# Slot lists one block ahead, layer weights in steps, and no empty openings in a sparse graph transformer

## Chip, cores and metric

The kernel runs on one core of one Trainium2 chip. The metric is device time in microseconds; before the change three runs gave 2359.41, 2360.68 and 2360.91 us, median 2360.68. The profile is one further execution, with a span of 2347.7 us. Below, PE is the matrix engine (TensorE), PEld its weight loads, DVE the vector engine, ACT the scalar engine, POOL the GpSimd engine, which here issues the gathers, and SP the engine that issues the plain DMAs.

## What is computed

Sixteen graphs share one adjacency of 1024 nodes with few edges (an edge with probability 0.0078, about 8 per row). Four layers follow each other: attention, graph attention, attention, attention. One attention layer is

```python
Q, K, V = h @ Wq, h @ Wk, h @ Wv              # 8 heads of 16
scores = Q K^T / sqrt(16), -inf where adj == 0
x = layer_norm(h + (softmax(scores) V) @ Wo + bo)
x = layer_norm(x + relu(x @ W1 + b1) @ W2 + b2)
```

and the graph attention layer takes `e = leaky(s_i + s_j)` from two projections of `h = x @ W`, a masked softmax over it, `att @ h + x`, and a layer norm. Everything is fp32.

## The kernel before

Because the adjacency is sparse, keys and values are not multiplied densely. In a setup phase (`graph`, L215 on) DVE counts the edges of every row, sorts the rows by degree, and finds for each sorted row the list of its neighbours. From then on the kernel gathers: per layer and graph group it keeps a table of 1024 rows with keys and values of 8 graphs, and fetches with indirect DMAs (L905, POOL) one table row per edge.

**Units.** There are 64 units (l, g, t), which the texts below call blocks and number from 0: 4 layers, 2 groups of 8 graphs, and 8 blocks t of 128 sorted nodes. Blocks 0 to 7 are layer 0 with the first group, 8 to 15 the second group. A block is cut into parts: 7 parts in t = 0, 5 in each other attention block. Per part DVE multiplies gathered keys with queries (L917), sums within heads (L940), and multiplies gathered values with the exponentials (L968); ACT takes the exponentials (L944); PE adds the edges of each node up with a 0/1 matrix `marks` (L984, accumulator `acc`). Once per block DVE divides (L1021, L1024; the denominators `ps` also come from L984).

**Slot lists.** Before a block can be gathered, `slots` (L382) must turn its neighbour lists into gather indices `idx` and into `marks`. `spread` (L384) does four small PE products (L387) into a PSUM bank; 18 small DVE instructions (L398 to L433) read that bank and write `idx` and `marks`.

**Tails.** Each block has two tails, one per half of its graphs (`attention_tail`, L662): transposes of o (L616), output projection (L680, L681), layer norm on ACT (L594 to L609), hidden layer (L691, ACT L700), second product (L705, L709), layer norm, transposes, and the projection into the next layer's table (L566 for the graph attention layer).

**Order of the work.** The order of instructions on each engine is fixed by the Python program: every engine executes its own in the order in which they were issued, and waits for others by semaphores. The main loop (L1110) issues DVE's part work and, between, calls `others()` three times per part, four in the graph attention layer. One such call is an *opening*. It advances the tails at a set pace, and then takes one step of the first generator in a queue: `fronts` if there are any, else `loads`, else the leisure work `slow`. In `fronts` stand slot lists, weights and the queries of the next block (L848: L868, ACT L872, L877, ACT L880); in `loads` stands `loaded` (L814), which fetches rows of x by an indirect DMA (L826, POOL) and transposes them (L616); in `slow` stands `at_leisure(1)` (L746), which projects keys and values of the second group (L616, L546) while the first group's blocks run. A step that only finds its generator at an end uses the opening up. Whatever is left in `fronts` at a block's end is issued there at once, and what is left in `slow` is issued before the first gather of block 8. PSUM results of PE rotate through a pool of four banks (`bank()`).

In the kernel before, `fronts` starts with all remaining slot lists, then the rows of block 1, then the weights of layer 0 and of the graph layer (L486 to L495 and L512 to L519); all of it must be issued within block 0. In `slots`, the products for the list after next are issued as soon as the bank has been read. The weights of layers 2 and 3 are worked on at the start of the fifth block of the layer ahead, all in one go (L1123).

Of the kernel before, what the change touches and what calls it, by code (L numbers as in the profile page):

```python
# [1 line left out]

# [1 line left out]

# [38 lines left out]
T = N // P  # L43
# [83 lines left out]
def sparse_path(ctx: ExitStack, tc: tile.TileContext, a: dict, out: bass.AP, flag):  # L127
# [254 lines left out]
    def slots():  # L382

        def spread(q):  # L384
            ps = bank([P, J, TOP])
            for j in range(J):
                nc.tensor.matmul(  # L387
                    ps[:, j, :], rep_of(j, True), lists[:, row_of(q, j), :],
                    start=True, stop=True,
                )  # L390
            return ps

        ps = spread(0)
        yield
        for q in range(T):
            for s in range(S):
                at = slice(32 * s, 32 * s + 32)
                nc.vector.tensor_copy(  # L398
                    val[at], ps[at].rearrange("p j (k s) -> p j k s", s=S)[:, :, :, s]
                )  # L400

            first, second = SHARED[q]
            for k in range(2):
                at = slice(32 * (2 + k), 32 * (3 + k))
                to, of = COUNT[q][first], S * COUNT[q][second] + k
                nc.vector.tensor_copy(val[at, first, to : to + 1], ps[at, second, of : of + 1])
            if 0 < q < T - 1:
                ps = spread(q + 1)

            def flat(v):  # L410
                return v.rearrange("p j k -> p (j k)")

            nc.vector.tensor_copy(flat(val_i), flat(val))

            for k, (by, op) in enumerate(
                ((2 * N - 1, ALU.bitwise_and), (11, ALU.logical_shift_right))
            ):
                nc.vector.tensor_scalar(flat(part), flat(val_i), by, None, op)
                nc.vector.tensor_scalar(
                    flat(idx[:, k, q]), flat(part), -1.0, float(N), ALU.mult, ALU.add  # L420
                )
            nc.vector.tensor_scalar(flat(used), flat(val), 0.0, None, ALU.is_gt)
            for j in range(J):
                c, n = MARK[q, j, 0], COUNT[q][j]
                nc.vector.tensor_tensor(
                    marks[:, c : c + n, :],
                    used[:, j, :n].rearrange("p (k o) -> p k o", o=1).to_broadcast([P, n, 32]),
                    mark32.to_broadcast([P, n, 32]),
                    ALU.mult,
                )  # L430
            for k in range(2):
                at, r = slice(64 * k, 64 * k + 64), COUNT[q][first]
                nc.vector.tensor_tensor(  # L433
                    marks[at, MARK[q, MIX, k], :],
                    used[at, first, r : r + 1].to_broadcast([64, 32]),
                    mark32[at, 0, :],
                    ALU.mult,
                )
            yield
            if q == 0:  # L440
                ps = spread(1)
                yield


    w = {}
# [12 lines left out]
    def load_weights(layer):  # L458

        t = wts.tile([P, 2 * D], F32, tag="Wkv", name="Wkv")
        nc.sync.dma_start(t[:, :D], a[f"{layer}_gnn_Wk"])
        nc.sync.dma_start(t[:, D:], a[f"{layer}_gnn_Wv"])
        w[layer, "Wkv"] = t
        yield
        for name in ATTN:
            src = a[f"{layer}_gnn_{name}"]
            if name in ("Wq", "Wo", "W1"):
                t = wts.tile([P, src.shape[1]], F32, tag=name, name=name)  # L470
                nc.sync.dma_start(t, src)
            elif name == "W2":
                t = wts.tile([P, F, D], F32, tag=name, name=name)
                nc.sync.dma_start(t, src.rearrange("(f p) d -> p f d", p=P))
            elif name == "b1":
                t = wts.tile([P, F], F32, tag=name, name=name)
                with nc.allow_non_contiguous_dma(reason="a bias, once"):
                    nc.sync.dma_start(t, src.rearrange("(f p) -> p f", p=P))
            elif name.startswith("ln") or name in ("b2", "bo"):
                t = wts.tile([P, 1], F32, tag=name, name=name)  # L480
                nc.sync.dma_start(t, src.rearrange("(p o) -> p o", o=1))
            else:
                continue
            w[layer, name] = t
        yield
        centred(w[layer, "Wo"], D)  # L486
        centred(w[layer, "W2"].rearrange("p f d -> p (f d)"), F * D)
        ps = bank([P, F])
        for f in range(F):
            nc.tensor.matmul(  # L490
                ps[:, f : f + 1], w[layer, "W1"][:, f * P : (f + 1) * P], w[layer, "b2"],
                start=True, stop=True,
            )
        nc.vector.tensor_tensor(w[layer, "b1"], w[layer, "b1"], ps, ALU.subtract)
        nc.vector.tensor_tensor(w[layer, "ln1_b"], w[layer, "ln1_b"], w[layer, "b2"], ALU.add)  # L495

# [2 lines left out]
    def load_graph_weights():  # L499
        for name in GAT[3:]:  # L500
            t = const.tile([P, 1], F32, name=name)
            nc.sync.dma_start(t, a[f"L1_gnn_{name}"].rearrange("(p o) -> p o", o=1))
            w["L1", name] = t

        nc.sync.dma_start(wg[:, :D], a["L1_gnn_W"])
        ends = const.tile([P, 2], F32, name="ends")
        for k, name in enumerate(("a_dst", "a_src")):
            nc.sync.dma_start(
                ends[:, k : k + 1], a[f"L1_gnn_{name}"].rearrange("(p o) -> p o", o=1)
            )  # L510
        yield
        ps = bank([P, P])  # L512
        nc.tensor.transpose(ps, wg[:, :D], ident)
        wgT = wts.tile([P, P], F32, tag="Wo", name="wgT")
        nc.vector.tensor_copy(wgT, ps)
        ps = bank([P, 2])
        nc.tensor.matmul(ps, wgT, ends, start=True, stop=True)
        nc.vector.tensor_copy(wg[:, D:], ps)
        centred(wg[:, :D], D)  # L519

# [293 lines left out]
    def loaded(u):  # L814

        if u >= len(units):
            return
        l, g, t = units[u]
        xs[units[u]] = inputs.tile([P, HF, GH, P], F32, tag="x", name="x")
        if l == 0:  # L820
            def fetch(h):
                if u == 0:
                    rows = twos.tile([P, GH, D], F32, tag="o", name="rows")
                else:
                    rows = ones_.tile([P, GH, D], F32, tag="q" if h else "rows", name="rows")
                nc.gpsimd.indirect_dma_start(  # L826
                    out=rows.rearrange("p g d -> p (g d)"), out_offset=None,
                    in_=a["x"].rearrange("n (k c) -> (n k) c", k=GR * HF),
                    in_offset=bass.IndirectOffsetOnAxis(ap=places[:, g, h, t : t + 1], axis=0),
                )  # L830
                return rows

            rows = fetch(0)
            yield "idle"
            yield "idle"
            turned(rows, xs[units[u]][:, 0])
            rows = fetch(1)
            yield "idle"
            yield "idle"
            turned(rows, xs[units[u]][:, 1])  # L840
            yield
            return
        nc.sync.dma_start(
            xs[units[u]].rearrange("p h g n -> p (h g n)"),
            kept[l, g][t].rearrange("p h c -> p (h c)"),
        )
# [192 lines left out]
    fronts = []  # L1039
# [18 lines left out]
    def others():  # L1058
        pace[0] += pace[1]
        while pace[0] >= 1.0:  # L1060
            advance(tails)
            pace[0] -= 1.0
        for gens in (fronts or loads or idle(),):
            if not gens:
                continue
            got = next(gens[0], "end")
            if got == "end":
                gens.pop(0)
            if got == "idle":
                advance(idle())  # L1070

    with tc.manual_schedule():
        wide = [gather_buffer() for _ in range(EDGES)]
# [30 lines left out]
            gathered(i)  # L1104
        nc.gpsimd.memset(wide[3], 0.0)
        gathered(AHEAD - 1)
        fronts.extend([rest, loaded(1)] + more)
        closing, sizes = None, ()
        begun = 0
        for i in range(len(parts) + 2):  # L1110
            here = i < len(parts)
            u = parts[i][0] if here else len(units)
            if here:
                l = units[u][0]
                if i and parts[i - 1][0] != u:
                    begun = i
                    if l + 1 < len(LAYERS) and LAYERS[l + 1][1] is ATTN:
                        if units[u][1:] == (0, 1):
                            more = load_weights(LAYERS[l + 1][0])
                            next(more)  # L1120
                            next(more)
                        if units[u][1:] == (0, 4):
                            next(more, None)  # L1123
                if is_attention(u):
                    products(i)
            if i > 1:
# [481 lines left out]
```

## Time and profile before

| engine | busy us of 2347.7 | share |
|---|---|---|
| PE matmul | 2066.7 | 88% |
| DVE | 1934.4 | 82% |
| ACT | 1530.3 | 65% |
| PE weight load | 1278.8 | 54% |
| POOL | 1084.9 | 46% |

DMA moved 636 MB, on average 271 GB/s. By slices of 58.7 us the busy tenths are not even (the page's second part):

| | slices 1 to 8 |
|---|---|
| PE | 7 5 4 7 9 9 8 8 |
| DVE | 7 8 7 7 7 8 6 6 |
| ACT | 3 2 1 5 7 7 7 7 |
| PE clock | 8 6 6 8 9 9 9 9 |
| DMA | 7 6 4 7 7 8 8 6 |

The setup phase ends at about 94 us; the third slice (117 to 176 us) lies in block 0. A block's length can be read from the times at which DVE starts L1021: block 0 closes at 186.7 us, block 1 at 235.2, block 2 at 277.5, block 7 at 500.1 and block 15 at 795.8. Rows of time give start, duration, engine, line, operation, what is written from what, size, number of merged instructions, and in brackets the idle time before it and what ended it. Rows of waits give the waiting instruction, what it waited for, the total, how often, and the longest.

### The profile page before, as it was taken

How to read it: one execution, taken by the hardware profiler on the slowest of the kernel's cores; microseconds unless marked ns; L12 is line 12 of the kernel's file. 1: busy time of each engine (PE TensorE's matmuls, PEld its weight loads, DVE VectorE, ACT ScalarE, POOL GpSimd, SP SyncE). 2: the span in 40 equal slices, each digit the busy share in tenths (PEclk: the TensorE clock that was granted, in tenths of full speed). 3: DMA queues.
4: the chain of work that ended last, by engine and by line, in shares of the span. 5: the costliest groups of instructions: out<-in, count | busy, mean ns of one | idle time of the engine just before them, and what ended most of it. 6: DMA issues, size and time to landing. Idle time of an engine off the chain costs nothing. (4 is left out here: it accounts for less than half of the span.)

```text
span 2347.7 us, 36598 instructions
## 1 busy us (share of the span) xinstructions
PE 2066.7 (88%) x13124; PEld 1278.8 (54%) x13124; DVE 1934.4 (82%) x1486; ACT 1530.3 (65%) x5057; POOL 1084.9 (46%) x754
## 2 busy tenths in 40 slices
PE   7547998879999899998899999999999989898987
PEld 6415665545655555554465665566555555455554
DVE  7877786689888677778898989889898888998884
ACT  3215777767777665565477876777767767676764
POOL 3334443344544568885333434343444445444441
PEclk8668999999999999999899999999999999999998
DMA  7647788668878889998888887888978677776760
GB/s 262 229 176 236 268 289 278 241 223 309 285 266 290 272 275 374 339 357 319 288 293 290 291 293 267 308 304 295 305 248 306 224 281 255 255 251 255 272 244 24
DMA packets 168461, 636.05 MB, mean 271 GB/s; under 512 B 38328, under 2 KB 41144, under 8 KB 119774
## 3 DMA queue, kind: packets, MB, share of 16 engines
q0 software_dynamic: 92672, 485.09, 57.7%
q1 hardware_dynamic: 75600, 148.55, 18.9%
q8 instruction: 105, 1.72, 0.3%
q14 instruction: 84, 0.69, 0.1%
HBM read 603.11 MB, written 92.34 MB: 296 GB/s over the span
## 5 line engine op out<-in xcount | busy, mean ns | idle before, releaser
L905 POOL DMA_INDIRECT e<-table,idx x600 | 879.5, 1466 | 1059.0 <-DVE pr L968 872.1
L968 DVE TENSOR_TENSOR pr<-e,ex 128x2048 f32<-128x2048 f32 (+1 forms) x336 | 689.3, 2060 | 54.0 <-ACT ex L944 32.1
L917 DVE TENSOR_TENSOR pr<-e,qr 128x2048 f32<-128x2048 f32 x204 | 460.6, 2258 | 184.5 <-DMA e<-table,idx 93.5
L984 PE MATMUL acc<-pr,marks 128*32 128x512 f32 x2656 | 536.8, 615 | 54.1 <-DVE pr L968 42.6
L940 DVE TENSOR_REDUCE sc<-pr 128x128 f32<-128x2048 f32 (+1 forms) x252 | 518.5, 2058 | 8.6
L594 ACT ACTIVATE z<-yps,root 128x128 f32<-128x128 f32 x888 | 317.4, 388 | 37.5 <-PE yps L709 20.6
L984 PEld LDWEIGHTS acc<-pr,marks 128*32 128x32 f32 x2656 | 109.3, 111 | 306.4 <-issue 216.1
L705 PE MATMUL yps<-W,f 128*128 128x128 f32 x1520 | 250.8, 282 | 9.3 <-ACT f L700 5.2
L609 ACT ACTIVATE z<-yps,rstd 128x128 f32<-128x128 f32 x888 | 254.0, 369 | 7.2
L705 PEld LDWEIGHTS yps<-W,f 128*128 128x128 f32 x1520 | 204.9, 192 | 57.3 <-ACT f L700 29.1
L546 PE MATMUL ps<-Wkv,xT 128*128 128x256 f32 x768 | 221.5, 430 | 15.9 <-ACT xT L622 9.5
L700 ACT ACTIVATE f<-ps,b 128x512 f32<-128x512 f32 x190 | 130.9, 693 | 159.6 <-PE ps L691 158.3
L880 ACT COPY qr<-ps 128x512 f32<-128x512 f32 x384 | 196.9, 599 | 44.6 <-PE ps L877 44.5
L877 PE MATMUL ps<-q,rep 32*128 32x512 f32 x768 | 174.4, 662 | 42.6 <-ACT q L872 40.9
L616 PE MATMUL ps<-ident,z 128*128 128x128 f32 x896 | 173.6, 297 | 36.4 <-ACT z L609 31.6
L944 ACT ACTIVATE ex<-sc 128x128 f32<-128x128 f32 (+1 forms) x252 | 79.7, 316 | 189.0 <-DVE sc L940 188.9
L594 ACT ACTIVATION_READ_ACCUMULATOR z<-yps,root 128x1 f32 x888 | 202.0, 227 | 0.0
L616 PEld LDWEIGHTS ps<-ident,z 128*128 128x128 f32 x896 | 113.9, 142 | 154.3 <-ACT z L609 84.3
L546 PEld LDWEIGHTS ps<-Wkv,xT 128*128 128x128 f32 x768 | 151.3, 211 | 79.8 <-ACT qr L880 24.3
L550 ACT COPY kv<-ps 128x512 f32<-128x512 f32 x176 | 103.4, 593 | 133.6 <-PE ps L546 130.7
L691 PE MATMUL ps<-x,W 128*128 128x512 f32 x384 | 188.8, 615 | 0.9 <-ACT x L624 0.9
L680 PE MATMUL yps<-Wo,oT 128*128 128x128 f32 x768 | 158.0, 288 | 9.6 <-ACT oT L622 9.6
(173 smaller groups left out, 2725.5 us busy)
## 6 DMA issues: line engine op xcount, KB each, us to landing
table<-kv SPq DMA_DIRECT2D x88, 512.0 KB, 6.9
qx<-qr SPq DMA_DIRECT2D x96, 256.0 KB, 5.3
kept<-xT SPq DMA_DIRECT2D x96, 256.0 KB, 3.3
x<-kept SPq DMA_DIRECT2D x48, 512.0 KB, 7.6
e<-table,idx POOLq DMA_INDIRECT x600, 7.8
table<-kv SPq DMA_DIRECT2D x32, 256.0 KB, 6.7
edges<-in_adj SPq DMA_DIRECT2D x8, 512.0 KB, 5.4
spare<-in_x SPq DMA_DIRECT2D x8, 512.0 KB, 7.9
```

The source lines that it names most:

```text
L546: nc.tensor.matmul(ps[:, k, :], x[:, i + k, :], w[LAYERS[l][0], "Wkv"], start=True, stop=True,)
L594: nc.scalar.activation(z[:, i, :], y[:, i, :], AF.Square, scale=D**-0.5, bias=root, accum_out=total[:, i : i + 1],)
L609: nc.scalar.activation(z[:, i, :], y[:, i, :], AF.Copy, scale=rstd[:, i : i + 1])
L616: nc.tensor.transpose(ps[:, i, :], z[:, i, :], ident)
L691: nc.tensor.matmul(ps, p["W1"][:, f * P : (f + 1) * P], x1.rearrange("p g n -> p (g n)"), start=True, stop=True,)
L705: nc.tensor.matmul(ps[:, i, :], f1[:, f, i * P : (i + 1) * P], p["W2"][:, f, :], start=(f == 0), stop=False,)
L880: nc.scalar.copy(qs[u][:, j, h * GH * D : (h + 1) * GH * D], pss[j])
L905: nc.gpsimd.indirect_dma_start(out=es[i][:, k, :], out_offset=None, in_=tables[l, g][:, :], in_offset=bass.IndirectOffsetOnAxis(ap=idx[:, ...
L917: nc.vector.tensor_tensor(prs[i][0][:, :n, :], es[i][:, :n, :ROW], qx[u].rearrange("p (o c) -> p o c", o=1) if (MIX, 0) in piece else of_p ...
L940: nc.vector.tensor_reduce(sc[:, :n, :], prs[i][0][:, :n, :].rearrange("p k (a d) -> p k a d", d=HD), mybir.AxisListType.X, ALU.add,)
L968: nc.vector.tensor_tensor(prs[i][k0 // 2][:, :m, :].rearrange("p k (a d) -> p k a d", d=d), es[i][:, k0 : k0 + m, base : base + ROW].rearr ...
L984: nc.tensor.matmul(outs[32 * j : 32 * j + 32], marks[:, mark, :], rhss, start=(chunk == mine[0]), stop=(chunk == mine[-1]),)
```

## The change

Five things are changed, all in the order of issue; the computation and the number of DVE and PE instructions of each kind stay as they are.

1. Slot lists are made a block ahead: list u + 1 is put into `fronts` at the start of block u (three steps of it, `islice(rest, 3)`), for u up to 6, instead of all lists in block 0.
2. Between the products of a list (`spread`) and the DVE instructions that read them lies one more opening. The products are no longer issued a list ahead.
3. The weights are worked on in steps: an opening is left between a product and DVE's reading of it (L490 to L494, L513 to L515, L517 to L518). For layers 2 and 3 this work is put into `fronts` instead of being issued in one go before the block's first L917.
4. Openings are dense: a generator that is at its end is dropped, and the opening goes to the next one.
5. In `loaded`, one more opening lies between the fetch of rows and their transposes, for both halves.

```diff
@@ slots
-        ps = spread(0)
-        yield
         for q in range(T):
+            ps = spread(q)
+            yield
+            if q:
+                yield
             for s in range(S):
...
-            if 0 < q < T - 1:
-                ps = spread(q + 1)
...
             yield
-            if q == 0:
-                ps = spread(1)
-                yield
@@ load_weights
+        yield
         nc.vector.tensor_tensor(w[layer, "b1"], w[layer, "b1"], ps, ALU.subtract)
@@ load_graph_weights
         nc.tensor.transpose(ps, wg[:, :D], ident)
+        yield
...
         nc.tensor.matmul(ps, wgT, ends, start=True, stop=True)
+        yield
         nc.vector.tensor_copy(wg[:, D:], ps)
@@ loaded, for both halves
             rows = fetch(0)
             yield "idle"
             yield "idle"
+            yield
             turned(rows, xs[units[u]][:, 0])
@@ others
-        for gens in (fronts or loads or idle(),):
+        while True:
+            gens = fronts or loads or idle()
             if not gens:
-                continue
+                break
             got = next(gens[0], "end")
             if got == "end":
                 gens.pop(0)
+                continue
             if got == "idle":
                 advance(idle())
+            break
@@ main loop
-        fronts.extend([rest, loaded(1)] + more)
+        fronts.extend([islice(rest, 3), loaded(1)] + more)
...
                     begun = i
+                    if u < T - 1:
+                        fronts.append(islice(rest, 3))
...
                         if units[u][1:] == (0, 4):
-                            next(more, None)
+                            fronts.append(more)
```

More of the change, by code (lines that the diff above doesn't have):

```diff
@@ L1 @@
 from contextlib import ExitStack
+from itertools import islice
 import numpy as np
@@ L839, in loaded @@
             yield "idle"
+            yield
             turned(rows, xs[units[u]][:, 1])
```

## The prediction

> **What bounds the kernel now.** I read the table of stretches first, cut where VectorE (DVE) closes a block (L1021), because the edit touches only the first sixteen blocks and two later spots. Columns: stretch, length, then busy time of PE, PEld, DVE, ACT and POOL, the granted PE clock, the DMA share and GB/s.
>
> ```profile
> 96.80:186.60 89.80, 41.01 (x181) 20.18 (x181) 75.44 (x165) 13.08 (x29) 27.58 (x19) 0.65 0.48 175
> 186.60:235.20 48.60, 40.38 (x241) 27.00 (x241) 32.40 (x19) 29.95 (x95) 19.97 (x15) 0.83 0.75 247
> 235.20:277.50 42.30, 38.02 (x254) 25.07 (x255) 32.40 (x18) 31.18 (x104) 17.77 (x13) 1.00 0.75 270
> 448.10:500.10 52.00, 40.38 (x253) 26.93 (x253) 32.59 (x19) 31.63 (x104) 15.24 (x12) 0.93 0.62 219
> 543.40:580.10 36.70, 33.86 (x230) 21.31 (x231) 32.21 (x18) 28.16 (x98) 19.66 (x14) 1.00 0.83 296
> ```
>
> Block 0 (first line) is DVE's: busy 75.4 of 89.8 us, while ACT and DMA are half empty. Blocks 2 to 6 of the first graph group (third line) take 42.3 us with DVE busy only 32.4 and PE 38.0; the same blocks of the second group (last line), which carry no leisure projection, take 36.7 with PE at 33.9 and the same DVE work. So those blocks follow PE, and DVE has about 10 us of slack in each. Block 7 (52.0) and block 1 (48.6) hold something extra.
>
> Next, the order in time of DVE in block 0 and the waits that end its idle time.
>
> ```profile
> 101.50 0.78 DVE L398 COPY little<-ps 32x24 f32<-32x24 f32 x4
> 104.39 0.38 DVE L433 TENSOR_TENSOR marks<-little 64x32 f32<-64x32 f32 x2
> 104.78 0.77 DVE L398 COPY little<-ps 32x24 f32<-32x24 f32 x4
> ...
> DVE pr L917 <- ACT qr L880: 6.6, 1, 6.6
> DVE b L494 <- PE ps L490: 4.0, 1, 4.0
> DVE wg L518 <- PE ps L517: 0.7, 1, 0.7
> ```
>
> One slot list takes 104.78 - 101.50 = 3.28 us of DVE, and seven stand in block 0. Three waits, 11.3 us, are DVE waiting for PE or ACT results whose instructions were issued only just before.
>
> Then the steady block, DVE and PE in order of time, and two waits of PE:
>
> ```profile
> 263.11 2.28 DVE L917 TENSOR_TENSOR pr<-e,qr 128x2048 f32<-128x2048 f32 x1
> 265.43 2.29 DVE L940 TENSOR_REDUCE sc<-pr 128x128 f32<-128x2048 f32 x1
> 272.25 2.29 DVE L968 TENSOR_TENSOR pr<-e,ex 128x2048 f32<-128x2048 f32 x1 [4.54 <-ACT ex L944]
> 277.55 0.56 DVE L1021 RECIPROCAL both<-ps 128x64 f32<-128x64 f32 x1 [3.00 <-PE ps L984]
> ...
> 267.93 1.91 PE L984 MATMUL acc<-pr,marks 128*32 128x512 f32 x8
> ...
> 191.55 1.08 PE L616 MATMUL ps<-ident,rows 128*128 128x128 f32 x4 [8.32 <-DMA rows<-in_x,places]
> 482.11 1.09 PE L616 MATMUL ps<-ident,rows 128*128 128x128 f32 x4 [6.76 <-DMA rows<-in_x,places]
> ```
>
> DVE runs ahead of PE by about 7 us at the block's start and then waits 7.5 us. The last two lines are the extra of blocks 1 and 7: PE stands still for rows of x that were asked for too late.
>
> **What the skill says.** "Perfetto Trace Analysis", Optimization Strategy: where the most contended engine changes over time, interleaving the regimes can pay. That is what the change does, and the table shows the two regimes. "TensorE: Matmul & The Clock Gate", The mechanism: matmuls start and end strictly in program order, so a spread put into PE's queue waits for all before it; the trace agrees (PE reaches the place of the new spread about 7 us after DVE). The same page, What's actually happening: the PE clock is halved after an idle window of about 3.4 us. Here the clock is 0.65 in block 0, and eight L984 took 3.63 us against 1.91 later. So PE work of block 0 is slow there, and PE prices from it are twice those of the busy blocks.
>
> **The change, part by part.**
>
> *Slots a block ahead.* By the built order, block 0 (cut at L1021) keeps the slot lists 1 and 2; lists 3 to 7 go one each to blocks 1 to 5. Block 0 loses 5 x 3.28 = 16.4 us of DVE, all on its bound. In a receiving block the list stands after the L968 that ended at 263.1 and before the L917 at 263.11. Its four spread matmuls stand on PE right after the accumulation of 267.93, so they run at about 269.8. Their cost: four took 1.87 us at half clock (L387), so I estimate 0.94 at full clock; bounds 0.6 (a row of four transposes, L616) and 1.87. PE is the bound there, so 0.94 is on the path, five times: +4.7. DVE waits at the list until 270.8, works to 274.1, and behind it are queued L917, L940 (to 278.6), L968 and L1021 (at about 281.2, against 277.55 + 0.94 without the list). The ex of that L940 is wanted by ACT at 275.98; ACT then idled for PE's L566 until 278.0, later plus 0.94, so it loses nothing. L1021 is 2.7 us late; its o is transposed at 282.3 + 0.94, still after it. The lateness ends in the next DVE wait (2 us for the accumulators, 10.0 us in five blocks) and the 4.5 us one. The spread holds one of four PSUM banks; its fourth successor (L566, 273.4) needs it back, and the six copies that free it end at about 272. So DVE's 3.3 us per block cost nothing, hidden in waits for PE.
>
> *Weights in steps.* In block 0 L494 and L518 get a DVE instruction of 2.3 us or more between matmul and reading: the waits of 4.0 and 0.7 go, -4. For layer 2 and 3 the step moves to an opening inside the loop. For layer 3 (L494 at 1246.85) L490 moves on PE behind an accumulation and a second product, 1.9 + 3.0 = 4.9 us, while L494 moves on DVE behind 4.6: the 2.84 us wait stays, 0. For layer 2 (L494 at 873.38) L490 moves behind an accumulation that took 3.63 us, L494 only behind 0.5 of small work: the wait grows from 1.8 to about 5. Behind it are an L968, and behind that the gather that waits for its buffer; DMA waits of 4 us follow, so I take +1.5 of the 3.1, bounds 0 and 3.
>
> *Dense openings and slots away: queries earlier.* The queries of block 1 now come one accumulation earlier in block 0, about 7 us, and the DVE wait of 6.6 for qr goes: -6.6. Against it, list 2 stands at the end of block 0 behind row transposes on a slow-clock PE: +4 (0 to 6). Block 0: -16.4 - 4 - 6.6 + 4 = -23.
>
> *One more opening before the row transposes.* In block 7 they now stand behind L705 and L691 of the other half. That is 2.7 + 1.9 = 4.6 us of PE work (the same rows in a steady block) inside the 6.76 it idled, and the clock need not fall (the L705 rows there took 4.2). DVE was held by a DMA until 481.48, and after it lost 1.65 (ex) and 3.34 (L1021) to PE: these 5.0 can go, I take -4.8. Block 8 is DVE's (42.7 of 43.3), so it keeps the lead. In block 1 the rows are asked for one gather earlier (12 gathers ahead instead of 13; the thirteenth waited 8.8 us on DVE): the 8.3 us stall goes and the block falls to the 42.3 of its neighbours, -6. Elsewhere the transposes fill the wait of L705 for ACT in one half instead of the other (0.4 us each): 0.
>
> Sum: -23 - 6 + 4.7 - 4.8 + 1.5 = -27.6, from 2360.7 to 2333.
>
> **Rivals.**
> *Block 0 finds another bound* (20%). Without the lists its parts follow at 6.9 us, each wants 2 MB of gathers, 290 GB/s, where the stage now moves 175; row transposes hold PE. For: two gathers took 10 us to land. Against: other stages move 296 to 356, and four buffers lie ahead. Then block 0 keeps half of its 23 and block 1 half of its 6: 2333 + 11.5 + 3 = 2347.
> *The work only moves* (5%). Each list costs its 3.3 us in its new block as well, and the stalls on rows stay: -16.4 - 10.6 + 16.4 + 4.7 + 1.5 = -4.4, 2356. The 10 us of DVE slack speak against it.
> *The list becomes the new wait* (9%, slower). DVE stops 6.7 us for the spread in five blocks, then works 3.3, and everything behind is late, gathers included: 5 x 10 = 50 instead of 4.7, with block 0 still -23, block 1 and 7 nothing gained, since POOL and PE wait on DVE, and 3 at layer 2: about +30, 2390; with half of it absorbed 2366. I take 2378. Against: the two DVE waits right behind the list are 7.5 us long and owed to PE anyway.
>
> **How the numbers follow.** Likeliest (66%) 2333. Its unknowns: the spread 5 x (0.6 to 1.9), list 2 (0 to 6), layer 2 (0 to 3), blocks 1 and 7 half or whole: 2318 to 2346. The range reaches into the first rival and a little beyond: 2318 to 2354. Faster by over 0.2% (under 2356) is the first two cases, 0.86; same is the third, 0.05; slower the last, 0.09.
>
> **What would show it.** Right: block 0 near 67 us with two lists in it; no wait of L917 on qr, nor of L494 there; blocks 2 to 5 about 43.2, with a DVE wait of some 7 us at L398 on L387 and shorter ones at L968 and L1021; block 7 near 47; L494 of layer 2 waiting 5 us. Wrong: blocks 1 to 5 above 45, block 0 above 75 with waits on gathers, or PE idle behind a PSUM bank that the list holds.

## The result and the profile after

The changed kernel took 2325.07 us (median of four, 2320.74 to 2332.53) against 2360.05 us (2353.03 to 2360.91) of the kernel before: a ratio of 0.9862, with a 95% interval of 0.9829 to 0.9895. Timed again later beside further kernels it took 2325.74 against 2351.28, ratio 0.9895 (0.9876 to 0.9914). The gain is thus 25 to 35 us; the two profiles differ by 28.8 us (2347.7 and 2318.9). The prediction said 2333 (2318 to 2354).

In the changed kernel most lines have moved by three: L917, L940, L968, L984, L1021 are now L920, L943, L971, L987, L1024, and the list is read at L401 and its products stand in L388. The table of stretches after, cut as before (stretch, length, busy time of PE, PEld, DVE, ACT, POOL, granted PE clock, DMA share, GB/s): block 0, block 1, block 2 and block 7.

```profile
97.25:169.80 72.55, 38.46 (x179) 18.12 (x179) 60.40 (x76) 14.05 (x31) 28.57 (x19) 0.74 0.61 229
169.80:213.20 43.40, 40.92 (x255) 26.49 (x252) 35.19 (x36) 30.64 (x100) 16.94 (x12) 0.93 0.75 266
213.20:254.90 41.70, 39.44 (x263) 26.03 (x260) 35.46 (x37) 31.13 (x104) 16.92 (x12) 1.00 0.78 275
420.00:465.90 45.90, 39.64 (x264) 26.14 (x262) 32.39 (x18) 32.63 (x111) 15.25 (x10) 1.00 0.69 250
```

Block 0 is 17.3 us shorter, block 1 5.2, block 7 6, and a block that now has a list in it is 0.6 us shorter than the same block before, though DVE works 3 us more there. DVE's waits in block 0 of the changed kernel (who waits, for what, total, times, longest):

```profile
DVE little L401 <- PE ps L388: 8.2, 1, 8.2
DVE pr L920 <- DMA e<-table,idx: 3.4, 1, 3.4
DVE b L493 <- PE ps L488: 2.7, 1, 2.7
```

The wait for qr (6.6 us before) is gone, that for the weights has fallen from 4.0 to 2.7, and a new one of 8.2 us stands at list 2. PE in order of time shows what list 2 waited for:

```profile
151.79 1.11 PE L617 MATMUL ps<-ident,rows 128*128 128x128 f32 x4 [7.60 <-DMA rows<-in_x,places]
152.70 1.91 PE L547 MATMUL ps<-Wkv,xT 128*128 128x256 f32 x4
154.54 4.06 PE L987 MATMUL acc<-pr,marks 128*32 128x512 f32 x8
158.54 1.07 PE L388 MATMUL ps<-little,rep 128*128 128x24 f32 x8
```

The list's products (last line) are queued behind row transposes whose rows had not landed. DVE stopped at 151.4, the rows landed at 151.8, and DVE's 8.2 us are the time in which PE worked off what stood behind them, at a clock of 0.50 until 154.5; the accumulation L987 took 4.06 us. Before, PE waited 8.3 us for the second half of the rows of block 2, at the start of block 1; now it waits 7.6 us for their first half, in block 0, and DVE pays for it at the list.

In the steady blocks the waits of PE tell the rest. Blocks 1 to 7 of the kernel before, the three largest:

```profile
PE ps L616 <- DMA rows<-in_x,places: 15.1, 2, 8.3
PE ps L566 <- ACT xT L624: 8.6, 7, 1.6
PE ps L546 <- ACT xT L622: 7.4, 7, 1.3
```

and the same of the kernel after (L567, L547 and L617 answer to L566, L546 and L616):

```profile
PE ps L567 <- ACT xT L625: 6.7, 7, 1.2
...
PE ps L547 <- ACT xT L623: 2.0, 2, 1.3
PE ps L617 <- DMA rows<-in_x,places: 1.5, 1, 1.5
```

In these blocks rows cost PE 1.5 us in place of 15.1. (In block 0, which PE does not bound, its waits for rows have grown from 4.9 to 31.4 us in all.) And the leisure projection L547, which waited about 1 us for ACT in every block, waits only twice: its transposes (`xg`) now stand ahead of an accumulation and not behind it.

The list itself, DVE and the end of block 2 in the kernel after:

```profile
244.76 0.77 DVE L401 COPY little<-ps 32x24 f32<-32x24 f32 x4 [5.60 <-PE ps L388]
...
254.89 0.56 DVE L1024 RECIPROCAL both<-ps 128x64 f32<-128x64 f32 x1
```

DVE now waits for PE once, at the list, 5.6 us, and no longer at L971 or L1024.

### The profile page after: what moved, and what is told of

Same layout as the page of the kernel before. It is cut to its first block, busy times and chain, and to the rows that moved or that the text cites. A ratio compares the mean times of both kernels' runs of the same rounds, so it can differ in the third digit from the quotient of the medians.

```text
span 2318.9 us, 36591 instructions
## 1 busy us (share of the span) xinstructions
PE 2064.1 (89%) x13124; PEld 1274.2 (55%) x13124; DVE 1933.8 (83%) x1486; ACT 1528.7 (66%) x5057; POOL 1091.8 (47%) x754
## 5 line engine op out<-in xcount | busy, mean ns | idle before, releaser
L971 DVE TENSOR_TENSOR pr<-e,ex 128x2048 f32<-128x2048 f32 (+1 forms) x336 | 689.2, 2060 | 21.8 <-ACT ex L959 16.1
L920 DVE TENSOR_TENSOR pr<-e,qr 128x2048 f32<-128x2048 f32 x204 | 461.8, 2264 | 160.5 <-DMA e<-table,idx 88.9
L987 PE MATMUL acc<-pr,marks 128*32 128x512 f32 x2656 | 537.0, 615 | 38.2 <-DVE pr L971 28.3
L943 DVE TENSOR_REDUCE sc<-pr 128x128 f32<-128x2048 f32 (+1 forms) x252 | 518.5, 2058 | 8.6
L987 PEld LDWEIGHTS acc<-pr,marks 128*32 128x32 f32 x2656 | 109.3, 111 | 291.1 <-issue 219.4
L547 PE MATMUL ps<-Wkv,xT 128*128 128x256 f32 x768 | 218.0, 426 | 12.7 <-ACT xT L623 4.3
L880 PE MATMUL ps<-q,rep 32*128 32x512 f32 x768 | 179.0, 656 | 47.3 <-ACT q L875 44.9
L617 PE MATMUL ps<-ident,z 128*128 128x128 f32 x896 | 175.6, 299 | 34.8 <-ACT z L610 29.9
L617 PEld LDWEIGHTS ps<-ident,z 128*128 128x128 f32 x896 | 114.6, 142 | 158.7 <-ACT z L610 85.8
L547 PEld LDWEIGHTS ps<-Wkv,xT 128*128 128x128 f32 x768 | 149.8, 209 | 70.4 <-ACT qr L883 19.8
```

Of the source, the lines that this page charges most:

```text
L547: nc.tensor.matmul(ps[:, k, :], x[:, i + k, :], w[LAYERS[l][0], "Wkv"], start=True, stop=True,)
L617: nc.tensor.transpose(ps[:, i, :], z[:, i, :], ident)
L920: nc.vector.tensor_tensor(prs[i][0][:, :n, :], es[i][:, :n, :ROW], qx[u].rearrange("p (o c) -> p o c", o=1) if (MIX, 0) in piece else of_p ...
L943: nc.vector.tensor_reduce(sc[:, :n, :], prs[i][0][:, :n, :].rearrange("p k (a d) -> p k a d", d=HD), mybir.AxisListType.X, ALU.add,)
L971: nc.vector.tensor_tensor(prs[i][k0 // 2][:, :m, :].rearrange("p k (a d) -> p k a d", d=d), es[i][:, k0 : k0 + m, base : base + ROW].rearr ...
L987: nc.tensor.matmul(outs[32 * j : 32 * j + 32], marks[:, mark, :], rhss, start=(chunk == mine[0]), stop=(chunk == mine[-1]),)
```

## The experiments

Each was timed beside the kernel before, in five rounds. The kernel before had medians from 2351 to 2360 us in the batches, so totals of different batches are best compared by their ratios. Lengths of blocks in us: block 0 from DVE's first product, the others from one L1024 (or its like) to the next. "2 to 5 by PE" is one block's mean when the cut is put at the end of the block's last product for the denominators (L984, L987), where PE's own pace is seen: a list makes DVE close its block about 3 us late, so by DVE's cut that lateness enters in the first block with a list and comes back in block 6. These means include blocks in which the PE clock fell. Block 19 is the one in which the weights of layer 2 are worked on.

| kernel | us | ratio (interval) | 0 | 1 | 2 to 5 by PE | 6 | 7 | 19 |
|---|---|---|---|---|---|---|---|---|
| before | 2351 to 2360 | 1 | 89.8 | 48.6 | 42.6 | 42.3 | 52.0 | 17.8 |
| after | 2325.07 | 0.9862 (0.9829-0.9895) | 72.5 | 43.4 | 42.2 | 38.8 | 46.0 | 19.9 |
| after, again | 2325.74 | 0.9895 (0.9876-0.9914) | 74.6 | 43.5 | 42.2 | 38.3 | 47.2 | 19.4 |
| lists undone | 2336.97 | 0.9928 (0.9900-0.9956) | 84.6 | 47.4 | 41.1 | 41.2 | 46.3 | 19.5 |
| lists alone | 2341.82 | 0.9947 (0.9923-0.9971) | 80.6 | 43.3 | 43.6 | 39.6 | 53.2 | 19.2 |
| rows undone | 2398.21 | 1.0186 (1.0151-1.0222) | 76.7 | 49.9 | 48.7 | 47.0 | 42.0 | 20.3 |
| dense undone | 2384.90 | 1.0114 (1.0082-1.0147) | 67.7 | 45.5 | 43.0 | 42.3 | 86.0 | 19.4 |
| weights undone | 2324.97 | 0.9888 (0.9863-0.9913) | 74.9 | 49.9 | 42.0 | 39.4 | 47.9 | 16.4 |
| slot opening undone | 2338.63 | 0.9937 (0.9912-0.9961) | 75.8 | 44.9 | 45.5 | 41.0 | 46.2 | 19.9 |
| lists two ahead | 2329.22 | 0.9908 (0.9881-0.9935) | 67.4 | 51.7 | 41.9 | 41.1 | 54.2 | 19.7 |
| the same, layer 2 as before | 2325.51 | 0.9890 (0.9862-0.9917) | 67.6 | 52.7 | 42.2 | 41.1 | 53.6 | 17.5 |
| after, layer 2 as before | 2320.63 | 0.9864 (0.9839-0.9889) | 73.2 | 43.3 | 42.2 | 38.3 | 46.9 | 16.9 |
| leisure in the third opening | 2334.81 | 0.9934 (0.9909-0.9959) | 76.5 | 49.8 | 44.8 | 41.8 | 36.7 | 20.8 |
| the same, layer 2 as before | 2336.62 | 0.9932 (0.9909-0.9956) | 73.1 | 50.6 | 46.1 | 41.2 | 36.7 | 18.1 |

**Lists undone.**

```diff
-        for q in range(T):
-            ps = spread(q)
+        ps = spread(0)
+        yield
+        for q in range(T):
...
-        fronts.extend([islice(rest, 3), loaded(1)] + more)
+        fronts.extend([rest, loaded(1)] + more)
...
-                    if u < T - 1:
-                        fronts.append(islice(rest, 3))
```

> The changed kernel with all slot lists back in block 0 and their products a list ahead (parts 1 and 2 undone, parts 3, 4 and 5 kept). Theory A: a list's four products cost PE about 1.07 us in each receiving block, and what shortens blocks 2 to 5 is another part, the openings, which put the leisure transposes ahead of the accumulation. Then block 0 gets five lists back (+16.4) but loses the 8.2 us in which DVE stood at list 2: 84 us instead of 75.8; blocks 2, 3 and 5 fall from 41.7 to 40.7; total +3, near 2328. Rival B: the products lie in waits of PE and cost nothing; blocks 2, 3 and 5 stay at 41.7 and the total is +8, near 2333. Rival C (the recorded sum): list 2 costs 4, so that undoing costs 16.4 - 4 - 4.7 = 7.7 with block 0 at 88.

Measured: +12 us. By PE a block of 2 to 5 takes 41.1 us without a list and 42.2 with one, 1.1 us more in the mean, as theory A said. But the blocks are not alike. Blocks 3 and 4 of the changed kernel, and then block 4 of this one, cut by PE:

```profile
251.79:293.45 41.66, 39.52 (x262) 26.05 (x261) 35.38 (x37) 31.25 (x104) 18.48 (x12) 1.00 0.78 273
293.45:336.42 42.97, 40.96 (x262) 27.56 (x261) 35.33 (x37) 31.60 (x104) 16.13 (x12) 0.96 0.78 277
313.84:355.02 41.18, 38.12 (x254) 25.02 (x253) 32.31 (x18) 31.08 (x104) 18.06 (x12) 1.00 0.82 289
```

Where the clock is 1.00 in both kernels a list costs 0.6 us (block 3: 41.66 against 41.06; block 5: 41.74 against 41.18): PE is busy 1.5 to 1.6 us longer and idle 0.9 to 1.1 us less. Block 2 pays 1.35, and block 4 pays 1.8, with a fall of the clock that this kernel does not have. So A's mean is right, but not as 1.07 us in each block.

A was too low on block 0: it expected 8.2 us more than in the changed kernel, and the block is 12.1 longer (84.6 against 72.5). To 16.4 for the lists comes a wait that A had left out, DVE for the queries,

```profile
DVE pr L923 <- ACT qr L886: 5.4, 1, 5.4
```

which is there again because seven lists stand ahead of the queries in `fronts`. So the dense openings alone do not remove the 6.6 us of the kernel before; the kernel with dense undone, below, shows that the lists' leaving alone does not remove them either. Block 1 also gets a stall of 4.3 us for rows.

**Lists alone** (the kernel before with parts 1 and 2).

```diff
         for q in range(T):
+            ps = spread(q)
+            yield
+            if q:
+                yield
...
+        fronts.extend([islice(rest, 3), loaded(1)] + more)
...
+                    if u < T - 1:
+                        fronts.append(islice(rest, 3))
```

> The kernel before with parts 1 and 2 alone (lists a block ahead, an opening between products and reading). Theory A: block 0 falls by 16.4 (five lists) and 6.6 (queries come earlier), and list 2 adds about 8, so 77 to 78 us instead of 92.7; the leisure transposes stay behind the accumulation, so blocks 2, 3 and 5 pay for the list's products, 42.3 + 1.07 = 43.3; block 7 keeps its stall on rows, 52. Total 2360 - 15 - 5 (block 1) + 4 = 2344. Rival B: moving the lists is itself what shortens blocks 2 to 5, so they show 41.7, and the total is near 2337.

Measured: 2341.82, near A. Blocks 2 to 5 pay for the list, 43.6 by PE against 42.6, and L544 (the leisure projection) still waits for ACT in all seven blocks, 7.3 us. So the 1 us that each steady block gained comes from parts 3 to 5, and the list costs 0.95 us in the mean. Again the mean hides the clock, which fell in blocks 3 and 4 here and only in block 4 of the kernel before; block 5, at 1.00 in both, is 0.55 us longer. Block 7 keeps its stall (53.2). Block 0 gained 9.2, not 15:

```profile
DVE little L401 <- PE ps L388: 10.3, 1, 10.3
DVE b L492 <- PE ps L488: 7.5, 1, 7.5
```

Both waits stand behind row transposes that waited 11.0 and 9.4 us for their rows. The sum closes: -16.4 (lists) - 6.6 (queries) + 10.3 (list 2) + 3.5 (weights, 7.5 in place of 4.0) = -9.2.

**Rows undone** (no extra opening before the row transposes, in both halves).

```diff
             yield "idle"
             yield "idle"
-            yield
             turned(rows, xs[units[u]][:, 0])
```

> The changed kernel without part 5 (no extra opening between the fetch of rows and their transposes). In the built order the leisure work (16 projections of the second group) then ends within block 6 (three of them there), and none is left for block 7, where the changed kernel has two in front of the first gather of block 8. Theory A: block 7 is set by these two, since the gather on POOL waits for the table they fill and the fetch of rows is queued behind it; then block 7 falls from 46 to about 38, block 6 gains 2.8, block 0 gains 1 to 2: total near 2321. Rival B (the recorded step): the extra opening is what hides the stall on rows in block 7; without it the 5 us come back, block 7 is 51, total near 2330.

Both theories missed: 73 us slower than the changed kernel, and slower than the kernel before. Blocks 1 to 6 and 8 to 13 are all longer, also in the second group, where no list is made (blocks 10 to 15 together 240.3 us against 216.5). PE's waits in blocks 2 to 5 have a line that the changed kernel does not have there, and the stretch of block 3 shows its second cost:

```profile
PE ps L617 <- DMA rows<-in_x,places: 15.6, 4, 4.2
```

```profile
276.50:324.80 48.30, 41.47 (x263) 26.63 (x260) 35.48 (x36) 31.14 (x104) 18.46 (x12) 0.93 0.68 235
```

Dense openings bring the transposes closer to the fetch (the kernel before, with neither dense openings nor the extra one, has no wait for rows in these blocks), so that PE stands about 4 us per block for rows. Its clock falls (0.93 in the mean, against 1.00 in the changed kernel): it is 0.53 in the 2 us behind the wait, and 0.65 and 0.50 once more from 316 to 320. PE's busy time is 1.9 us longer: 4.2 + 1.9 is 6.1 of the 6.6 that block 3 lost. "TensorE: Matmul & The Clock Gate", What's actually happening, in the Trainium skill, says that the clock halves after an idle window of about 3.4 us; the wait of 4.2 us agrees. The second fall does not come from such a window: no wait before it is above 1.13 us (more of this in the last section). What A said of block 7 came true in part, 42.0 with no leisure work in it, but the rows held it too.

**Dense undone.**

```diff
-        while True:
-            gens = fronts or loads or idle()
+        for gens in (fronts or loads or idle(),):
             if not gens:
-                break
+                continue
             got = next(gens[0], "end")
             if got == "end":
                 gens.pop(0)
-                continue
...
-            break
```

> The changed kernel without part 4 (an opening at which a generator ends is used up again). In the built order blocks 1 to 6 then hold one leisure projection each instead of two, and nine stand in block 7 ahead of the first gather of block 8. Theory A: the dense openings pay for the openings that lists and rows now take; without them blocks 2 to 6 fall by about 2.8 each and block 7 grows by seven projections of 3.2 us, with DVE standing for it: block 7 near 68, total +5 to +8, near 2331. Rival B: dense openings matter only for the queries of block 1 (6.6 us of DVE in block 0); then block 0 is 82, block 7 stays near 46 and the total is near 2332.

Measured: +60. A named the main cause and undersized it. Nine leisure projections stand in front of the first gather of block 8, and DVE waits for the accumulation behind them; the second fence is the last of the nine on PE:

```profile
486.41 2.29 DVE L920 TENSOR_TENSOR pr<-e,qr 128x2048 f32<-128x2048 f32 x1 [44.74 <-PE acc L987]
```

```profile
479.11 3.63 PE L547 MATMUL ps<-Wkv,xT 128*128 128x256 f32 x8 [0.73 <-ACT xT L623]
```

One after the other they take 4.7 us each on average and not 3.2: four of them wait about 2 us for their own load, and three run on a slow clock (3.4 to 3.6 us for L547 in place of 1.99). Blocks 1 to 6 did not fall by 2.8 each with half the leisure work: together they are 11 us longer than in the changed kernel (261.3 against 250.2). Blocks 10 to 15, which have no leisure work, grew by 14 us (230.5). In a block of the second group PE waited 1.94 us at L567 where the changed kernel waits 0.87, and ran at half clock for a while after; the waits of PE with leisure work, L547 for ACT, are back (5.4 us in five blocks). In blocks 2 to 6 PE's waits sum to some 21 us in place of 9.5, and its clock is 0.88 to 0.96 in four of the five, where the changed kernel has 1.00 in four. Why ACT comes later there is not settled.

In block 0, which is 5 us shorter, the waits at list 2 and for the weights are gone, and another is back:

```profile
DVE pr L920 <- ACT qr L883: 5.6, 1, 5.6
```

So the wait for qr needs both parts, lists away and dense openings, as the prediction had it; B had this wait right, and neither the length of block 0 nor the total. (With lists alone it is gone too, but there DVE has stood 17.8 us in other waits before it.)

**Weights undone.**

```diff
-        yield
         nc.vector.tensor_tensor(w[layer, "b1"], w[layer, "b1"], ps, ALU.subtract)
...
-                            fronts.append(more)
+                            next(more, None)
```

> The changed kernel with the weights as before (part 3 undone: no opening between a product and DVE's reading of it, layers 2 and 3 in one go ahead of the block's first products). Theory A: in block 0 DVE waits for the weight products again, about 5 us in place of 2.7, so block 0 is longer by 2 to 3; layer 2 gets its 2 us back (block 19 falls from 19.9 to about 17.8, the wait of the weights from 3.6 to 1.8). Sum near 0 to +1: 2325 to 2326. Rival B (the recorded step): -4 and +1.5 undone, that is +2.5, 2328. Rival C: the openings that the weights take in block 0 matter through what else moves (leisure work, rows), and the total changes by more than 6 either way.

No difference that the total shows (2324.97; A). Block 0 is 2.4 us longer with a wait of 5.0 for the weights, block 19 3.5 shorter. Block 1 is 6.5 us longer (a wait of 3.5 for ACT and a clock of 0.85), since the weights take fewer openings and what stands behind them moves: C's mechanism. Blocks 0 to 15 together are 8 us longer (676.2 against 668.2 and 668.5 in the two profiles of the changed kernel), more than A's 2 to 3, and the interval of the total, about 6 us either way, is too wide to show it.

**Slot opening undone.**

```diff
             yield
-            if q:
-                yield
...
-        fronts.extend([islice(rest, 3), loaded(1)] + more)
+        fronts.extend([islice(rest, 2), loaded(1)] + more)
...
-                        fronts.append(islice(rest, 3))
+                        fronts.append(islice(rest, 2))
```

> The changed kernel without part 2 (one opening, not two, between a list's products and DVE's reading). Theory A: PE's order in blocks 2 to 6 is the same, DVE only reaches the list one opening (about 4.5 us) earlier and waits that much longer, in slack that PE owns: blocks 2, 3 and 5 stay at 41.7, the wait at the list there is 8 to 10 us in place of 5.9; in block 0, where DVE is the bound, list 2 costs up to 4.5 more. Total +0 to +4, near 2327. Rival B: the longer stop delays gathers behind it and blocks 1 to 5 grow by 2 or more each: near 2337.

B in its size, +13 and blocks 2 to 5 at 45.5 by PE, but not by its path: DVE waits for no gather in blocks 2 to 6. PE's order is the same, but DVE takes the list one opening earlier, and must do the L969 of one part and the whole of the next after it. Block 3 at its end, ACT and then PE:

```profile
309.79 0.31 ACT L945 ACTIVATE ex<-sc 128x128 f32<-128x128 f32 x1 [4.36 <-DVE sc L941]
...
310.73 0.64 ACT L873 COPY q<-ps 128x512 f32<-128x512 f32 x1
```

```profile
311.42 1.13 PE L878 MATMUL ps<-q,rep 32*128 32x512 f32 x6 [2.02 <-ACT q L873]
```

ACT waits for the sums of the last part, the copy of the next block's q is queued behind, and PE waits for that copy; after these gaps its clock is 0.56 and 0.58 in the two stretches from 314 to 318 us. Of the 3.3 us that a block of 2 to 5 lost, 1.8 are more idle time of PE and 1.5 more busy time. This is the rival "the list becomes the new wait", in that what is queued behind the list comes late. In the changed kernel the same PE wait is 0.7 to 1.3 us: the list fits, but by less than one opening.

**Lists two ahead**, and the same with the weights of layers 2 and 3 done in one go.

```diff
-        fronts.extend([islice(rest, 3), loaded(1)] + more)
+        fronts.extend([islice(rest, 6), loaded(1)] + more)
...
-                    if u < T - 1:
+                    if u < T - 2:
```

> The changed kernel with list 2 made right behind list 1 in block 0, and every later list two blocks ahead (six steps in block 0, one list per block up to block 4). Theory A: the 8.2 us in which DVE stood at list 2 were spent behind row transposes on PE whose rows had not landed; list 2's products now stand right behind list 1's, and list 3's come at the block's end in its place, so the wait only goes if nothing else holds that place. In the built order the accumulation and no row transposes stand ahead of list 3's products, so its wait falls to 2 us or less, while one more list is in block 0 (+3.3): block 0 by 3 us shorter, one list fewer behind, and one leisure projection more in block 7 (+4) for one fewer in block 1 (-2.8): total -2, near 2323. Rival B: the wait was for PE's slow clock and its accumulation; then it stays at 8, and the total is +4, near 2329.

> The same, with the last step of the weights of layers 2 and 3 done in one go ahead of the block's first products, as before the change. Theory A: block 19 falls by 2.1 against the run before it, since PE has the product ahead of the accumulation again; layer 3 moves by less than 1: near 2321. Rival B: the gathers set block 19 (DMA waits of 1 to 3 us stand behind that wait), and the total is that of the run before.

The wait at the list is gone from block 0, which is 5 us shorter though it holds a third list: A's view of the 8.2 us holds. An accumulation as slow as before (3.62 us) still stands ahead of the list's products, but no row transposes do, so B's clock and accumulation alone do not make the wait. The total does not fall. Block 1 is longer (51.7 in place of 43.4): PE waits for rows just before it and for ACT in it,

```profile
162.58 1.08 PE L617 MATMUL ps<-ident,rows 128*128 128x128 f32 x4 [4.34 <-DMA rows<-in_x,places]
...
186.30 2.07 PE L547 MATMUL ps<-Wkv,xT 128*128 128x256 f32 x4 [3.47 <-ACT xT L623]
```

and in block 7 (54.2), which has a third leisure projection and a DVE wait of 16.2 us in place of 8.4. With layer 2 as before the change, block 19 is 2.2 us shorter; the totals' intervals overlap.

**After, again, and three versions.** Layer 2 as before:

```diff
-                            fronts.append(more)
+                            for _ in more:
+                                pass
```

Leisure in the third opening:

```diff
             yield "idle"
             yield "idle"
-            yield
+            yield "idle"
             turned(rows, xs[units[u]][:, 0])
```

> The changed kernel itself, unchanged, timed beside the next three on the same chip: 2325, within 4.

> The changed kernel with only the last step of the weights of layers 2 and 3 done in one go, ahead of the block's first products, as before the change; the weights of layer 0 and of the graph layer keep their steps. Theory A: block 19 falls by 2 to 3.5 (the two runs that had this showed 17.5 and 16.4 in place of 19.9), and block 35 changes by less than 1: the total falls by 2, to near 2323. Rival B: what block 19 gains is lost in the blocks behind it, which follow the gathers; no change.

> The changed kernel with the extra opening of part 5 also given to the leisure work. In the built order three of the sixteen leisure projections stand in block 1, two in each of blocks 2 to 6 and none in block 7. Theory A: block 7 is set by the two projections ahead of the first gather of block 8 and by the gathers that wait for their table, so it falls from 46 to about 38, with DVE's waits of 8.4 us for the accumulation and of 4.9 us for the gather gone; blocks 0 and 1 grow by 3 to 5 together: total -3, near 2322. Rival B: block 7 is set by the rows alone (1.5 us of waiting left), so it falls only by the two projections' 5 us of PE work, which block 1 and block 0 take over: no change, 2325.

> Both edits at once: if they don't touch each other, the sum of the two, near 2320; block 7 near 38 and block 19 near 17.5.

The changed kernel timed again took 2325.74, as expected. With layer 2 as before, block 19 falls from 19.4 to 16.9, as expected. DVE's wait for the weights in the changed kernel, second profile, and then in this one:

```profile
847.05 0.16 DVE L493 TENSOR_TENSOR b<-b,ps 128x2 f32<-128x2 f32 x1 [4.94 <-PE ps L488]
```

```profile
842.96 0.16 DVE L493 TENSOR_TENSOR b<-b,ps 128x2 f32<-128x2 f32 x1 [2.39 <-PE ps L488]
```

The time, 2320.63, is the lowest of all, 5 us under the changed kernel beside it, but the intervals overlap (0.9839 to 0.9889 and 0.9876 to 0.9914): that block 19 is faster is shown, that the total is faster is not. Nor do the two profiles show it beyond that block: blocks 16 to 31 together take 309.9 us with this edit and 308.8 without, so what block 19 gains is lost in the blocks behind it, which is B. The other version did to block 7 what A said, 36.7 in place of 47.2 with no leisure work left in it, and lost more elsewhere: block 1 +6, blocks 2 to 6 +15, where PE now waits 7.3 us for the loads of `xg` and its clock is 0.93 to 0.96 in all five (1.00 in four of the five in the changed kernel). Neither of its two theories had that. With both edits the sum doesn't come out either.

## Why the prediction was right

The time landed 8 us under the likeliest value, and the two profiles differ by 28.8 us where the sum said 27.6. The sum was nearly right with terms that were not: errors of both signs met, and that is luck.

- **Block 0, -23; measured -17.3** (-15.2 in the second profile). The lists' -16.4 and the queries' -6.6 came as written. The step on list 2 failed, "+4 (0 to 6)" for "row transposes on a slow-clock PE": it is 8.2, and 10.1 in the second profile. The slow clock was there, but the step left out that the rows themselves land late: PE stood 7.6 us for them, until after DVE had stopped, and all that was queued behind them fell into DVE's wait. The step on the weights, "-4", was -2.0: 2.7 us of wait are left, since L488 too stands behind row transposes, which waited 3.5 us.
- **Block 1, -6 + 0.94; measured -5.2.** Right in size; but PE's stall for rows has not gone, it has a counterpart of 7.6 us in block 0.
- **Lists in blocks 1 to 5, +0.94 each.** The mean came near: 0.95 in the kernel with lists alone, 1.1 between the changed kernel and the one with lists undone, and the four products took 1.07 us. In part that is luck: with the clock at 1.00 in both kernels a list costs 0.55 to 0.6 us (blocks 3 and 5), since PE's idle time shrinks as well; block 2 pays 1.35, and the means hold a fall of the clock that the kernel beside does not have. The step had no term for these. DVE's stop at the list is 5.6 to 6.3 us, where the step's own times (263.1 to 270.8) give 7.7. That DVE's 3.3 us are hidden was right with the two waits named, and nearer its limit than the text said: one opening earlier and the list sets the block.
- **"Elsewhere ... 0" was wrong.** Dense openings put the leisure transposes ahead of an accumulation, and PE's 1 us wait for ACT in each block went: 41.1 by PE against 42.2, lists aside (blocks 2, 3, 5 and 6 of the kernel with lists undone and of the kernel before). So blocks 2, 3 and 5 show 41.7 and not the 43.2 predicted. The step priced the move of the row transposes and left out that of `xg`, which the built order shows as well.
- **Block 7, -4.8; measured -6.0** (-4.8 in the second profile). The wait for rows fell from 6.8 to 1.5. But "it keeps the lead" was wrong: blocks 8 and 9 gave back 2.9 (1.2 in the second profile). DVE waits 7.5 us for PE and ACT there in place of 4.6; PE stands 3.1 us for rows in block 8 in place of 1.6, and its clock is 0.96 there in place of 1.00.
- **Layer 2, +1.5; measured +2.1** in block 19 (+1.6 in the second profile), with a wait of 3.6 us behind a gather wait of 1.8; in the second profile it is 4.9, near the 5 that were said.
- **The rivals.** None set the time. Of the first, row transposes holding PE are what the 8.2 us at list 2 are; its gathers are not seen (3.4 us of wait in block 0, 3.6 before). The third came, though not by gathers, as soon as one opening was taken away. What all cases missed is that the parts don't add: undoing rows or dense alone costs 73 or 60 us, more than the whole change gains.

## What to carry to other kernels

In a program whose order is fixed by turns, an edit that gives or takes a turn moves everything behind it; price edits together, from the built order, and look at each kind of work that moves, not at the ones the edit names. Work put into another engine's slack is free only while nothing that feeds the bound engine is queued behind it, so follow the chain one more engine (here DVE, ACT, PE) and count what margin is left. And cut blocks at the engine that sets the pace: by DVE's cut blocks 2 to 6 took 206.7 us with lists and 206.0 without, as if a list were nearly free; by PE's they took 210.0 and 205.7. Look at the clock of each block before taking a mean for a price.

## What was unexpected of the hardware

The PE clock fell without a long gap. In block 11 of the kernel with dense undone PE's longest wait was 1.94 us, ending at 671.4, and the clock then read as follows, in stretches of 2 us (columns as in the table of stretches; the clock is the third number from the end):

```profile
668.00:670.00 2.00, 1.46 (x8) 0.45 (x4) 1.56 (x1) 2.00 (x11) 1.07 (x2) 1.00 0.04 4
670.00:672.00 2.00, 0.60 (x4) 0.52 (x4) 1.29 (x1) 1.94 (x10) 0.00 (x0) 1.00 0.43 131
672.00:674.00 2.00, 1.98 (x13) 0.92 (x14) 1.00 (x1) 1.97 (x9) 0.73 (x1) 0.90 0.93 242
674.00:676.00 2.00, 2.00 (x14) 0.61 (x12) 0.00 (x0) 0.24 (x2) 1.25 (x2) 0.50 1.07 210
```

In the 4 us from 668 to 672 PE was busy for 2.06; the clock then fell, to 0.90 and 0.50 in the next two stretches. In the same block of the changed kernel, where the wait is 0.87 us, the clock stays at 1.00. But the length of one wait does not decide it: in block 3 with rows undone the clock is 0.65 and 0.50 from 316 to 320 us with no wait above 1.13 us before it, and in block 4 of the changed kernel 0.71 and 0.50 from 298 to 302 us, after waits of 0.92 and 0.67. So the clock fell without an idle window of 3.4 us, and in these cases short waits cost their own length and then some clock. How much idle time it takes was not measured.

DVE's first product, at the end of a setup phase whose code is nearly the same in all, started between about 96 and 104 us in the fourteen profiles, and layers 2 and 3 took 1238 to 1250 us with little changed in them. Totals of single runs therefore differ by some us for reasons outside the blocks that were edited, which is why the blocks are compared above.
